# One x tile per block in the v stage, the squares' norms in a tile of their own pool, and another order of the first loads of a 7x7 stage

## The chip, the cores and the metric

The kernel runs on one NeuronCore of a Trainium2 chip. The time is that of one execution on the device, in microseconds (us): the median of three runs. A NeuronCore has five engines with instruction streams of their own: TensorE (PE; its weight loads are PEld in the profile), VectorE (DVE), ScalarE (ACT), GpSimd (POOL) and SyncE (SP). Each carries out its stream in order and waits on semaphores that the others or transfers raise. SP does nothing here but issue transfers (DMAs); ACT and POOL issue some beside their other work. All transfers run on the same 16 DMA engines. PE writes into PSUM, a small memory of banks; everything else lies in SBUF, 128 partitions wide.

## The reference

The input x is (1, 384, 192, 192), all in float32. Two layers follow each other, each `x + layer(group_norm(x))`:

```python
x = x + conv_attention(_gn(x), ...)      # layer 0
x = x + dwconv7x7(_gn(x), symmetrised weight)   # layer 1
# layer 0:
qkv = einsum('bchw,oc->bohw', x, w_qkv)          # 384 -> 1152 channels
qkv = qkv.reshape(b, 3*c, 96, 2, 96, 2).max(axis=(3, 5))   # 2x2 max pool
qkv = depthwise 3x3 convolution of qkv           # 'SAME', 1152 groups
q, k = rows of q and k divided by their norms over all 9216 positions
attn = einsum('bhcn,bhdn->bhcd', q, k)           # 8 heads, 48x48, over channels
out = sum over four k of a_i * topk_softmax(attn, k) @ v
out = upsample2x(gelu(out)); out = einsum with w_proj
```

The norms of q and k need every position, so v is used only after q and k are complete. The second group norm needs all of layer 0's output.

## The kernel before, in words

**Statistics.** x is read once for the first group norm, and the scale is folded into the weights `wq`. Convolutions of the first q/k blocks are begun meanwhile.

**q/k stage** (loop `for b in range(NB + 1)`, NB = 24 blocks of 8 image rows). For each of six channel tiles `pooled` multiplies (L639) into PSUM tile `pq` and pools on DVE into a `ring` tile; one block later `depthwise` runs nine taps on DVE (L680, L682) into `qk`; `products` squares qk on ACT (L691, sums into `ssq`), transposes it on PE (L700), copies it out on ACT (L706) and adds to the Gram matrices (L709). In the last round (b == NB) there is no new block. `convolve` then begins the v convolution (L537) of the first four x tiles from `xv_begun`, two tiles and one channel tile at a time, six calls of twelve matmul passes; they are called after channel tiles 2, 4 and 6, ahead of the last `products`.

**v stage.** A block (NBC = 16) is two rows of every 32, so a block has NT = 6 tiles of 2x192 positions for each of KT = 3 channel tiles. `load_v` loads two of the tiles (UT = 2) by three DMAs on SP (L880); `convolve` multiplies and reduces 2x2 maxima on DVE (L543) into `rows`; `depthwise_v` adds nine taps on DVE (L907 for the first, L903) into `vb`; `attend` multiplies with the attention matrix (L959) and applies gelu on ACT (L966); `project` multiplies with `w_proj` (L983), and ACT writes y (L991). `residual` adds x, loaded once more by `load_r` (L1000), to y in four DVE additions (L1017) into one of three `sx` tiles, squares the sum on ACT (L1037) for the second group norm, and stores it to the DRAM tile `sd` from POOL (L1058, two DMAs of 600 KB) and for edge rows to `sh`. All x tiles, for the convolution and for the residual, come from one pool `xp2` of six buffers with one tag. Three blocks are convolved ahead while `attention` runs, a generator whose steps are called between the convolutions: it makes the norms `rn` from `ssq` (L771 to L781, with one power on POOL), spreads them along the free axis by diagonal tiles `dg` and a matmul (`along_free`, L223 to L225), scales the Gram matrices (L788), ranks the entries on DVE (L813 to L821) and builds the softmax mix. Its tiles are in pool `ap`. Then the loop over i runs in a written order; behind it come the last three blocks without convolutions: all taps still missing, then three rounds of attend, project and residual.

**7x7 stage.** 48 steps of CB = 8 channels. A step n needs `main` (the rows, 1200 KB, from sd), `aux` (edge rows, 600 KB, from sh), `w` (1024 KB) and `h` (256 KB), each with three buffers, filled two steps ahead from ACT's queue; steps 0 and 1 are loaded from SP. POOL's `borders` prepares main and aux, ACT's `columns` and `rest` copy parts of w into h and of main into aux, DVE's `middle` adds the residual's diagonal to w. `h` also gets a row of constants, `offs`, which DVE makes from the second group norm (L1294, L1299) and ACT's queue writes by DMA (L1296, L1300). Then PE takes, for each of eight channels, three matmuls into `pc` (L1389, L1394 with w and main, L1400 with h and aux), and DVE and ACT scale the result out (L1413, L1411); POOL interleaves it (L1359) and SP stores it (L1363). `along` spreads means and scales as above through PSUM tiles of the same tag `pc`.

**What sets the order.** A planner orders each engine's stream by the order in which the program is traced and by when it expects inputs to be ready. `keep` (also given as `pin`) ties an instruction behind the one traced before it on its engine; `with tc.issue_after(ins)` ties a group behind `ins` on its engine. A pool's memory is taken as a stack; a tile of a new pool waits for those who used the memory before. `multiplied` is the last Gram matmul of the latest `products`.

Of the kernel before, what the change touches and what calls it, by code (L numbers as in the profile page):

```python
# [78 lines left out]
def conv_preact_d2(  # L79
# [138 lines left out]
    def along_free(dst, src, pool, name, tag=None):  # L218

        ps = pool.tile([P, C], F32, name=f"af_{name}", tag=tag or f"af_{name}")  # L220
        for t in range(KT):
            dg = const.tile([P, P], F32, name=f"dg_{name}_{t}", tag="dg", bufs=2)
            nc.vector.tensor_scalar_mul(dg, ident, src[:, t : t + 1])  # L223
            nc.tensor.matmul(ps[:, t * P : (t + 1) * P], ones, dg, start=True, stop=True)
# [305 lines left out]
    def convolve(i, t0, ct, xb, pin):  # L530
# [3 lines left out]
        for u in range(UT):  # L534
            for kt in range(KT):
                pin(
                    nc.tensor.matmul(  # L537
                        ps[:, u, 0 : RB * HW], wq[:, kt, o : o + P], xb[:, kt, u, :],
# [12 lines left out]
    with ExitStack() as bx:  # L551
# [172 lines left out]
        for b in range(NB + 1):  # L724
# [3 lines left out]
            else:  # L728
# [3 lines left out]
                xb = xpool.tile([P, KT, 2 * UT, RB * HW], F32, name="xv_begun", tag="xb")  # L732
                for kt in range(KT):
                    nc.sync.dma_start(xb[:, kt], image_rows(kt, order[0], 0, 2 * UT))
            qk = []
            for ct in range(2 * KT + 1):
# [10 lines left out]
                if b > 0 and ct > 0:  # L747
# [3 lines left out]
                    if b == NB and ct % 2 == 0:  # L751
                        for n in range(ct - 2, ct):
                            t0 = n // KT * UT
                            convolve(0, t0, n % KT, xb[:, :, t0 : t0 + UT], lambda ins: ins)
                    if ct == 2 * KT:
                        multiplied = products(b - 1, qk)
            if b == 2:
# [10 lines left out]
    def attention(ap):  # L768

        rn = ap.tile([P, 2 * KT], F32, name="rn")  # L770
# [98 lines left out]
    xp2 = dx.enter_context(tc.tile_pool(name="xp2", bufs=6))  # L869
# [6 lines left out]
    def load_v(i, t0):  # L876
        b = order[i]
        xb = xp2.tile([P, KT, UT, RB * HW], F32, name=f"xv{b}_{t0}", tag="xv")
        for kt in range(KT):
            nc.sync.dma_start(xb[:, kt], image_rows(kt, b, t0, UT))  # L880
# [117 lines left out]
    def load_r(i, ot):  # L998
        xr = xp2.tile([P, NT, RB * HW], F32, name=f"xr{order[i % NBC]}_{ot}", tag="xv")
# [108 lines left out]
    for j, dys in ((NBC - 2, (2,)), (NBC - 1, (0, 1)), (NBC, (0,))):  # L1108
# [3 lines left out]
    for j in range(NBC - 2, NBC + 1):  # L1112
        gl = attend(j, keep)
        after = []
        for ot in range(KT):
# [5 lines left out]
            next(after[ot])  # L1121
        before = after
# [13 lines left out]
    with ExitStack() as ex_:  # L1136
# [24 lines left out]
        def queue(n):  # L1161

            if n < 2:
                return nc.sync.dma_start
            return lambda dst, src: keep(nc.scalar.dma_start(dst, src))
# [34 lines left out]
        ws = {n: load_w(n) for n in range(2)}  # L1200
        ws = {n: (ws[n], load_h(n)) for n in range(2)}
        auxes = {n: load_aux(n) for n in range(2)}
        mains = {n: (load_main(n), auxes[n]) for n in range(2)}
# [91 lines left out]
        for n in ws:  # L1295
            nc.scalar.dma_start(ws[n][1][ONE : ONE + 1], offs[span(n), 0, :])  # L1296
# [184 lines left out]
```

## Time and profile before

| what | value |
|---|---|
| three runs, us | 2817.28, 2816.37, 2819.05 (median 2817.28) |
| the profiled execution, us | 2823.79 |
| its span, first to last instruction, us | 2822.1 |
| mean granted PE clock | 0.987 |
| busy: PE, PEld, DVE, ACT, POOL, us | 2640.9, 1582.7, 2320.9, 870.5, 761.4 |
| moved by DMA | 584.52 MB, 207 GB/s on average |
| q/k stage ends, v stage begins | about 1360 to 1394 us |
| loop of the v stage | blocks of 50.35 us, to 2141 us |
| last three blocks | 2142 to 2217 us |
| 7x7 stage | from 2229.78 us, 48 steps, 11.64 us each |

The profiled execution is 6.5 us longer than the median of the runs; sums made from the profile's durations are made against the profiled execution. Matmuls in float32 appear as two passes each, so "x12" is six matmuls. Times in "start us" are counted from the span's start. In a row of waits the numbers are the total, how often, and the longest. A wait for several semaphores is put down to the one that came last by the profile.

### The profile page before, as it was taken

Reading aid. Unit: us, or ns where it says so; the run is one execution under the profiler, and the core shown is the slowest. Engines: PE = TensorE matmul, PEld = TensorE weight load, DVE = VectorE, ACT = ScalarE, POOL = GpSimd, SP = SyncE. Lnnn points to the kernel's source line nnn. Section 1 sums busy time; section 2 is a strip of 40 time slices with the busy share of each in tenths; the row PEclk is TensorE's granted clock in tenths of the full one; section 3 lists DMA queues with packets and bytes.
Section 4 is the critical chain, followed back from the end, with each engine's and each line's share of the span. In section 5 each row is a group of like instructions: output and inputs, shape, how many; then the busy total and the mean of one; then the engine's idle time right before and its main releaser. Section 6 shows DMA issues by size and latency. Waiting matters only on the chain.

```text
span 2822.1 us, 25467 instructions
## 1 busy us (share of the span) xinstructions
PE 2640.9 (94%) x8671; PEld 1582.7 (56%) x8671; DVE 2320.9 (82%) x3382; ACT 870.5 (31%) x1637; POOL 761.4 (27%) x884
## 2 busy tenths in 40 slices
PE   0399999999999999999999999999998699999997
PEld 0144444444445444444556666666666477777775
DVE  7989887887878878778698888888889678777886
ACT  0141111111111111111202232322324567777775
POOL 1034444100000000000102230100101467888886
PEclk9999999999999999999999999999999799999999
DMA  9976766301001011010235998575666899999997
GB/s 377 400 244 219 258 200 219 126 34 67 34 34 67 34 51 50 34 67 1 80 124 189 332 376 293 199 251 179 235 207 224 301 304 362 372 373 370 373 373 248
DMA packets 236353, 584.52 MB, mean 207 GB/s; under 512 B 16656, under 2 KB 168064, under 8 KB 219456
## 3 DMA queue, kind: packets, MB, share of 16 engines
q1 hardware_dynamic: 175296, 286.77, 29.1%
q0 software_dynamic: 37376, 148.85, 15.2%
q10 hardware_dynamic: 23552, 147.27, 13.9%
q8 instruction: 69, 1.13, 0.2%
q14 instruction: 60, 0.49, 0.0%
HBM read 374.47 MB, written 208.21 MB: 206 GB/s over the span
## 4 chain that ended last, share of the span: by engine, by line
PE 89%; DVE 6%; DMA 3%; POOL 1%; issue 1%; ACT 0%; ACTq 0%; POOLq 0%; SPq 0%; DVEq 0%
PE pq L639 38%; PE pv L537 18%; PE pc L1400 6%; PE pc L1389 6%; PE pc L1394 6%; PE pr L983 4%; PE po L959 3%; DMA xs<-in_x_dram 2%; PE grams L709 2%; PE tr L700 2%; PE pq_begun L423 1%; DVE st L318 1%; DVE vb L903 1%; DVE sx L1017 1%; DMA bp<-in_bproj_dram 1%
## 5 line engine op out<-in xcount | busy, mean ns | idle before, releaser
L639 PE MATMUL pq<-xq,wq 128*128 128x512 f32 x2268 | 990.7, 592 | 0.0
L639 PEld LDWEIGHTS pq<-xq,wq 128*128 128x128 f32 x2268 | 423.2, 190 | 492.0 <-issue 446.8
L682 DVE SCALAR_TENSOR_TENSOR qk<-ring,wd,qk 128x384 f32<-128x384 f32 x1152 | 676.1, 615 | 20.9 <-ACT ring L669 7.1
L537 PE MATMUL pv<-xv,wq 128*128 128x384 f32 x1656 | 540.7, 487 | 3.2 <-DVE rows L543 3.0
L647 DVE TENSOR_REDUCE ring<-pq 128x128 f32<-128x512 f32 x428 | 294.7, 689 | 190.5 <-PE pq L639 188.8
L537 PEld LDWEIGHTS pv<-xv,wq 128*128 128x128 f32 x1656 | 314.8, 190 | 218.3 <-DVE rows L543 5.0
L1413 DVE TENSOR_SCALAR apart<-pc,rb 32x576 f32<-32x576 f32 x384 | 312.0, 813 | 125.7 <-PE pc L1400 111.4
L1411 ACT ACTIVATE apart<-pc,rb 32x576 f32<-32x576 f32 x384 | 281.1, 732 | 144.5 <-PE pc L1400 139.7
L903 DVE SCALAR_TENSOR_TENSOR vb<-rows,wd,vb 128x576 f32<-128x576 f32 x384 | 313.3, 818 | 11.3
L1400 PE MATMUL pc<-aux,h 128*128 128x288 f32 x768 | 250.9, 408 | 2.7 <-POOL aux L1322 2.7
L1389 PE MATMUL pc<-main,w 128*128 128x288 f32 x768 | 251.4, 409 | 0.3 <-issue 0.3
L1394 PE MATMUL pc<-main,w 128*128 128x288 f32 x768 | 251.3, 409 | 0.0
L1017 DVE TENSOR_TENSOR sx<-xr,y 128x576 f32<-128x576 f32 x192 | 217.4, 1173 | 33.8 <-ACT y L991 21.4
L691 ACT ACTIVATE junk<-qk 128x384 f32<-128x384 f32 x144 | 75.3, 523 | 548.8 <-DVE qk L682 548.8
L801 POOL MEMSET lower<- 128x2304 f32 x1 | 2.0, 2017 | 881.1 <-ACT rows L508 881.1
L1359 POOL COPY res<-apart 128x1152 f32<-128x1152 f32 x96 | 210.0, 2222 | 87.2 <-DMA out_dram<-res 61.0
L1058 POOL DMA_DIRECT2D sd<-sx x96 | 72.2, 756 | 491.8 <-DVE sx L1017 474.2
L543 DVE TENSOR_REDUCE rows<-pv 128x192 f32<-128x768 f32 x144 | 137.8, 957 | 54.2 <-PE pv L537 54.1
L1400 PEld LDWEIGHTS pc<-aux,h 128*128 128x128 f32 x768 | 146.3, 191 | 45.5 <-POOL aux L1322 3.5
L1394 PEld LDWEIGHTS pc<-main,w 128*128 128x128 f32 x768 | 146.7, 191 | 41.9
L1389 PEld LDWEIGHTS pc<-main,w 128*128 128x128 f32 x768 | 146.4, 191 | 41.9 <-issue 0.6
L1037 ACT ACTIVATE wq<-sx,negmid 128x1152 f32<-128x1152 f32 x96 | 120.6, 1256 | 96.6 <-DVE sx L1017 92.5
(216 smaller groups left out, 2384.5 us busy)
## 6 DMA issues: line engine op xcount, KB each, us to landing
sd<-sx POOLq DMA_DIRECT2D x96, 600.0 KB, 10.1
xr<-in_x_dram SPq DMA_DIRECT2D x48, 1152.0 KB, 14.1
out_dram<-res SPq DMA_DIRECT2D x192, 288.0 KB, 8.4
main<-sd ACTq DMA_DIRECT2D x46, 1200.0 KB, 9.8
xv<-in_x_dram SPq DMA_DIRECT2D x138, 384.0 KB, 5.4
xq<-in_x_dram SPq DMA_DIRECT2D x21, 2304.0 KB, 8.2
w<-wt ACTq DMA_DIRECT2D x46, 1024.0 KB, 6.6
xs<-in_x_dram SPq DMA_DIRECT2D x24, 1536.0 KB, 15.1
```

The source lines that it names most:

```text
L537: nc.tensor.matmul(ps[:, u, 0 : RB * HW], wq[:, kt, o : o + P], xb[:, kt, u, :], start=(kt == 0), stop=(kt == KT - 1),)
L639: nc.tensor.matmul(ps, wq[:, kt, ct * P : (ct + 1) * P], rows[:, kt, :, g * 64 : (g + 1) * 64], start=(kt == 0), stop=(kt == KT - 1), skip ...
L647: nc.vector.tensor_reduce(t[:, r0 : r0 + PR, 1 + g * 32 : 1 + (g + 1) * 32], ps.rearrange("p (h a w b) -> p h w a b", h=PR, a=2, b=2), AX. ...
L682: nc.vector.scalar_tensor_tensor(dst, src, w, dst, ALU.mult, ALU.add)
L903: pin(nc.vector.scalar_tensor_tensor(dst, src, w, dst, ALU.mult, ALU.add))
L1017: nc.vector.tensor_tensor(bass.AP(flat.tensor, flat.offset + at(e) + a * RUN, [flat.ap[0], [JP, NT], [1, NJ], [at(f) - at(e), 2]],), xq[:, ...
L1359: keep(nc.gpsimd.tensor_copy(res[:, k], apart[:, :, k].rearrange("p e n -> p n e")))
L1389: nc.tensor.matmul(acc, w[:, i, 0:P], main[:, i, :, 0:NJ], start=True, stop=False)
L1394: nc.tensor.matmul(acc, w[:, i, P : 2 * P], main[:, i, :, 1 : 1 + NJ], start=False, stop=False,)
L1400: nc.tensor.matmul(acc, h[:, i], aux[:, i, :, 0:NJ], start=False, stop=True,)
L1411: keep(nc.scalar.mul(dst, src, scale))
L1413: keep(nc.vector.tensor_scalar_mul(dst, src, scale))
```

## The change

*In q/k's last round and in attention.* `along_free` has one `dg` buffer for each of its three diagonal tiles instead of two in all. `rn` comes from the pool `const` instead of `ap`. The begun convolutions are called at other channel tiles: two after the third, two after the fifth, one after the sixth, one after the seventh round, and all under `issue_after(multiplied)`: the first five are tied behind the last Gram matmul of block 22, the sixth behind that of block 23. `xv_begun` has the tile index ahead of the channel tile.

*In the v stage.* One tile `xvs` in a pool `xvp` holds the x of a whole block; `load_v` fills a third of it, with the tile index ahead of the channel tile. `xp2` has three buffers, for the residuals' x alone. For the last block but one of those that are finished (i == NBC - 1) `load_r` returns a view of `xvs`, whose content is still there, and issues no load: three DMAs of 1152 KB fewer. The first three taps of the last block finished, (NBC, ct, 0) for three ct, move from before the last three rounds to behind the second residual of their first round.

*Into the 7x7 stage.* The loads of steps 0 and 1 on SP are tied to the program's order, behind the last `load_r`, and their order is now w 0, h 0, h 1, aux 0, main 0, w 1, aux 1, main 1; before it was w, h, aux, main, each for both steps. The three DMAs of `offs` are issued from SP instead of ACT. In step 0 the first two pairs of channels take their w and main matmuls, eight in all, before the first h and aux matmul; the other steps keep their order.

```diff
-            dg = const.tile([P, P], F32, name=f"dg_{name}_{t}", tag="dg", bufs=2)
+            dg = const.tile([P, P], F32, name=f"dg_{name}_{t}", tag="dg", bufs=KT)
...
-                xb = xpool.tile([P, KT, 2 * UT, RB * HW], F32, name="xv_begun", tag="xb")
+                xb = xpool.tile([P, 2 * UT, KT, RB * HW], F32, name="xv_begun", tag="xb")
                 for kt in range(KT):
-                    nc.sync.dma_start(xb[:, kt], image_rows(kt, order[0], 0, 2 * UT))
+                    nc.sync.dma_start(xb[:, :, kt], image_rows(kt, order[0], 0, 2 * UT))
...
-                    if b == NB and ct % 2 == 0:
-                        for n in range(ct - 2, ct):
-                            t0 = n // KT * UT
-                            convolve(0, t0, n % KT, xb[:, :, t0 : t0 + UT], lambda ins: ins)
                     if ct == 2 * KT:
                         multiplied = products(b - 1, qk)
+                    if b == NB:
+                        with tc.issue_after(multiplied):
+                            for n in ((), (), (0, 1), (), (2, 3), (4,), (5,))[ct]:
+                                t0 = n // KT * UT
+                                convolve(0, t0, n % KT, xb[:, t0 : t0 + UT], lambda ins: ins)
...
-        rn = ap.tile([P, 2 * KT], F32, name="rn")
+        rn = const.tile([P, 2 * KT], F32, name="rn")
...
-    xp2 = dx.enter_context(tc.tile_pool(name="xp2", bufs=6))
+    xp2 = dx.enter_context(tc.tile_pool(name="xp2", bufs=3))
+    xvp = dx.enter_context(tc.tile_pool(name="xvp", bufs=1))
+    xvs = xvp.tile([P, NT, KT, RB * HW], F32, name="xv")
...
-        b = order[i]
-        xb = xp2.tile([P, KT, UT, RB * HW], F32, name=f"xv{b}_{t0}", tag="xv")
+        xb = xvs[:, t0 : t0 + UT]
         for kt in range(KT):
-            nc.sync.dma_start(xb[:, kt], image_rows(kt, b, t0, UT))
+            nc.sync.dma_start(xb[:, :, kt], image_rows(kt, order[i], t0, UT))
...
+        if i == NBC - 1:
+            return xvs[:, :, ot]
+        xr = xp2.tile([P, NT, RB * HW], F32, name=f"xr{order[i % NBC]}_{ot}", tag="xr")
...
-    for j, dys in ((NBC - 2, (2,)), (NBC - 1, (0, 1)), (NBC, (0,))):
+    for j, dys in ((NBC - 2, (2,)), (NBC - 1, (0, 1))):
...
+            if (j, ot) == (NBC - 2, 1):
+                for ct in range(KT):
+                    depthwise_v(NBC, ct, (0,), keep)
...
-            if n < 2:
-                return nc.sync.dma_start
-            return lambda dst, src: keep(nc.scalar.dma_start(dst, src))
+            engine = nc.sync if n < 2 else nc.scalar
+            return lambda dst, src: keep(engine.dma_start(dst, src))
...
-        ws = {n: load_w(n) for n in range(2)}
-        ws = {n: (ws[n], load_h(n)) for n in range(2)}
-        auxes = {n: load_aux(n) for n in range(2)}
-        mains = {n: (load_main(n), auxes[n]) for n in range(2)}
+        ws, mains = {0: load_w(0)}, {}
+        hs = [load_h(n) for n in range(2)]
+        for n in range(2):
+            ws[n] = ws[n] if n == 0 else load_w(n), hs[n]
+            aux = load_aux(n)
+            mains[n] = load_main(n), aux
...
-            nc.scalar.dma_start(ws[n][1][ONE : ONE + 1], offs[span(n), 0, :])
+            nc.sync.dma_start(ws[n][1][ONE : ONE + 1], offs[span(n), 0, :])
...
-        nc.scalar.dma_start(wh[ONE - TOP].rearrange("(t p) n -> p t n", p=P), offs)
+        nc.sync.dma_start(wh[ONE - TOP].rearrange("(t p) n -> p t n", p=P), offs)
...
+            def sums(q, steps):
+                if q not in ahead:
+                    ahead[q] = pc.tile([P, 2, 512], F32, name=f"pc{n}_{q}", tag="pc")
+                for k in range(2):
+                    i = 2 * q + k
+                    for j in steps:
+                        lhs, rhs = (
+                            (w[:, i, j * P : (j + 1) * P], main[:, i, :, j : j + NJ]) if j < 2
+                            else (h[:, i], aux[:, i, :, 0:NJ])
+                        )
+                        keep(
+                            nc.tensor.matmul(
+                                ahead[q][:, k, 0 : NT * NJ], lhs, rhs,
+                                start=(j == 0), stop=(j == 2), skip_group_check=True,
+                            )
+                        )
+                return ahead[q]
+
+            if n == 0:
+                for q in range(2):
+                    sums(q, range(2))
+            for q in range(CP):
+                ps = sums(q, range(2 if q in ahead else 0, 3))
```

More of the change, by code (lines that the diff above doesn't have):

```diff
@@ L537, in convolve @@
                     nc.tensor.matmul(
[L538 removed]
+                        ps[:, u, 0 : RB * HW], wq[:, kt, o : o + P], xb[:, u, kt, :],
                         start=(kt == 0), stop=(kt == KT - 1),
@@ L998, in load_r @@
     def load_r(i, ot):
-        xr = xp2.tile([P, NT, RB * HW], F32, name=f"xr{order[i % NBC]}_{ot}", tag="xv")
+        if i == NBC - 1:
+            return xvs[:, :, ot]
+        xr = xp2.tile([P, NT, RB * HW], F32, name=f"xr{order[i % NBC]}_{ot}", tag="xr")
         nc.sync.dma_start(xr, image_rows(ot, order[i % NBC], 0, NT))
@@ L1382, in conv_preact_d2 @@
             apart = outp.tile([P, CP, 2, NT * NJ], F32, name=f"apart{n}", tag="apart", bufs=3)
-            for q in range(CP):
-                ps = pc.tile([P, 2, 512], F32, name=f"pc{n}_{q}", tag="pc")
+            ahead = {}
+            def sums(q, steps):
+                if q not in ahead:
+                    ahead[q] = pc.tile([P, 2, 512], F32, name=f"pc{n}_{q}", tag="pc")
                 for k in range(2):
                     i = 2 * q + k
-                    acc = ps[:, k, 0 : NT * NJ]
-                    keep(
-                        nc.tensor.matmul(
-                            acc, w[:, i, 0:P], main[:, i, :, 0:NJ], start=True, stop=False
-                        )
-                    )
-                    keep(
-                        nc.tensor.matmul(
-                            acc, w[:, i, P : 2 * P], main[:, i, :, 1 : 1 + NJ],
-                            start=False, stop=False,
-                        )
-                    )
-                    keep(
-                        nc.tensor.matmul(
-                            acc, h[:, i], aux[:, i, :, 0:NJ],
-                            start=False, stop=True,
-                        )
-                    )
+                    for j in steps:
+                        lhs, rhs = (
+                            (w[:, i, j * P : (j + 1) * P], main[:, i, :, j : j + NJ]) if j < 2
+                            else (h[:, i], aux[:, i, :, 0:NJ])
+                        )
+                        keep(
[3 more added lines that the diff above has]
+                            )
+                        )
+                return ahead[q]
[4 more added lines that the diff above has]
+                ps = sums(q, range(2 if q in ahead else 0, 3))
                 c = n * CB + 2 * q
```

## The prediction

> **What bounds the kernel now.** I read the page's chain first, then PE's waits, then the stages in which those waits lie. The chain says who has to be relieved:
>
> ```profile
> PE 89%; DVE 6%; DMA 3%; POOL 1%; issue 1%; ACT 0%; ACTq 0%; POOLq 0%; SPq 0%; DVEq 0%
> ```
>
> PE is the bound, and the other 11% lie where PE is let down. The list of who waited for whom, for PE, names the places (total, times, longest, in us). Leaving out the statistics at the start, which the change does not touch, they are few:
>
> ```profile
> PE po L959 <- DVE vb L903: 5.1, 2, 3.6
> PE af_rk L224 <- DVE dg_rk L223: 3.9, 1, 3.9
> PE pv L537 <- DVE rows L543: 3.0, 1, 3.0
> PE pc L1400 <- POOL aux L1322: 2.7, 1, 2.7
> ```
>
> Next the busy time by stretch (start and end; length; PE, PEld, DVE, ACT, POOL busy; granted PE clock; DMA share; GB/s): one block of the v loop, the moment after the wait of af_rk, the sums at the end of the v stage, the first matmuls of the 7x7 stage.
>
> ```profile
> 1800.25:1850.60 50.35, 50.35 (x173) 32.70 (x173) 44.81 (x51) 13.76 (x30) 4.48 (x6) 1.00 0.63 215
> 1401.09:1404.51 3.42, 3.23 (x9) 2.45 (x10) 1.24 (x4) 0.00 (x0) 0.00 (x0) 0.50 0.84 279
> 2176.00:2217.00 41.00, 22.57 (x96) 16.87 (x94) 33.53 (x35) 27.01 (x57) 10.48 (x14) 0.83 1.01 367
> 2229.00:2241.00 12.00, 8.99 (x20) 5.87 (x20) 4.00 (x8) 3.13 (x3) 7.14 (x11) 0.51 0.73 278
> ```
>
> The v loop is PE without a hole (50.35 of 50.35), so whatever the change does inside it is worth nothing unless it makes PE wait. At the v stage's end PE is half idle and the DMA engines are full (1.01). Around the first and the last of these stretches PE runs at half clock. So the change is priced in three seams.
>
> **Seam 1, from q/k to v (1360 to 1447).** The chain in order of time (start, us):
>
> ```profile
> 1393.02 1.22 ACT rows L508 x5
> 1394.27 2.02 POOL lower L801
> 1396.29 1.33 POOL rn L772
> 1399.08 2.06 DVE dg_rk L223
> 1401.28 1.19 PE af_rk L224 x4
> ```
>
> The squares that rn sums were done on ACT at 1381.1, but rn was reduced at 1394.35, right after the last gram matmul: it waits for memory that the q/k stage still held under pool `ap`, and on POOL it then stands behind the memset of `lower`. In `const` that wait is gone: the reduce can go at 1381, the power (1.36), the maximum (1.0) and the reciprocal (0.2) by about 1385, ten us before PE asks. The third diagonal, which waited 0.76 for PE with two buffers, has its own. PE's 3.89 go, and with them the half clock: 3.23 us of matmul at 0.50, worth 1.6. Attention's comparisons on DVE (15 of 2.55 us) start some ten us earlier, so they needn't be run back to back; the 3.05 wait at 1446.8 comes where three follow each other (1438.40, 1440.95, 1443.41) with no `rows` reduce between. I count it as gone; if the order keeps such a triple, it stays. Together 8.5.
>
> Against it stands the new order of the first six convolutions. Before, twelve of their passes (2, 4, 4 and 2 in PE's timeline from 1361.55 to 1368) filled the holes between the transposes of block 22, whose copies on ACT stand behind squares that wait for DVE (1.84 us idle before 1363.61). Now they are queued behind that block's last gram matmul; nothing else is there for PE, and 12 passes at 0.3225 (the chain has 36 in 11.61) = 3.9 come back as idle time. From both sides: 0 if ACT's order closes up, 3.9 if not; I take 3.9, as the row stands. The sixth convolution moves behind the last gram matmul, a swap that costs PE nothing and brings the grams 3.9 forward; ACT's border fills of `rows2` (18 of 0.26) move behind it and have no reader before block 3 at 1487. **Net 4.6.**
>
> The loads: SyncE's first v load waited for the last depthwise (DVE, 1380.35) and then
>
> ```profile
> SPq L880 <- PE pv L537: 8.1, 1, 8.1
> ```
>
> for the begun convolutions, until 1388.5. The new tile follows a halved xp2 in the stack, so by the pools' sizes it lies over the rings and not over the q/k x tiles: about 8 us earlier. Nothing waited for these loads before; this covers the sixth convolution's move, after which the next input is wanted at once (otherwise 5.4 us from issue to landing would be bare).
>
> **The v loop.** Three loads of 384 KB per pair of tiles as before, the same 1536-byte runs. A third of the tile is free once its own convolution of the previous block is done, 38.6 us before it is wanted (1800.2 to 1838.8), against 5.4 to land; a residual's x comes one block ahead as before, 14.1 against more than 30. DVE has 5.5 us to spare. Zero; without that cover a late load costs PE directly, in 12 blocks.
>
> **Seam 2, the last three blocks (2142 to 2217).** Here DVE sets the end: 33 depthwise taps of 0.82 (27.1), then nine sums of four L1017 at 1.17 started 1.14 apart (4.55 each, 41.0): 2142.0 + 68.1 = 2210.1. The last ended at 2217.0; the 6.9 between are
>
> ```profile
> DVE sx L1017 <- DMA sd<-sx: 5.5, 4, 2.2
> DVE sx L1017 <- ACT wq L1037: 1.5, 1, 1.5
> ```
>
> since sum n+3 needs the buffer of sum n, whose stores take 9 to 12.8 us to land. Moving nine taps (7.4) behind the second sum lets the first two start 7.4 earlier, and the taps run while their stores land. The third sum starts at 2178.2, as before (2177.98), and its store opens the sixth, that one's the ninth. So the gain isn't 7.4: it is what these two stores gain in a full DMA. From 2183 until the sixth store was in, the engines had about 9.6 MB to move (four and a half stores of 1.23, two x loads of 1.18, h and both aux); now 8.3 (the half store and one x load are in earlier, one aux queues behind `main` 0, `w` 0 comes in). 1.3 MB at the row's 367 GB/s is 3.5. Three x loads (3.5 MB) of the kept block go too, but at 2133 to 2157, where they held up nobody. **3.5**, between 0 (the ninth waits as long) and 6.9 (no wait left). What is late next: `w` 0 and `w` 1, loaded at 2159 while the DMA idled, are pinned into the full stretch; 1 MB is 2.9 us, counted above for `w` 0, and `w` 1 goes behind `main` 0.
>
> **Seam 3, into the 7x7 stage.** ACT stood still for the constant's rows, and so the copies for the third tap group came late:
>
> ```profile
> 2231.46 0.62 ACT L1187 COPY h<-w 32x512 f32<-32x512 f32 x1 [13.02 <-DVE offs L1299]
> 2232.53 2.12 ACT L1349 COPY aux<-main 32x2304 f32<-32x2304 f32 x1
> ```
>
> ACT's end (2234.65), and not POOL's as the wait says (borders done 2231.45), released L1400:
>
> ```profile
> 2229.78 1.30 PE L1389 MATMUL pc<-main,w 128*128 128x288 f32 x2 [0.30 <-issue]
> 2234.74 1.30 PE L1400 MATMUL pc<-aux,h 128*128 128x288 f32 x2 [2.70 <-POOL aux L1322]
> 2240.63 0.72 PE L1400 MATMUL pc<-aux,h 128*128 128x288 f32 x2
> 2241.19 0.65 PE L1389 MATMUL pc<-main,w 128*128 128x288 f32 x2
> ```
>
> With the rows on SyncE these copies end near 2228.5, and eight matmuls that need neither aux nor h go first (8 x 0.97 = 7.8 at half clock), so the 2.7 close. The rest is clock. Eight matmuls were done at 2240.63; at full clock (0.485) they take 3.9, so the stage began in effect at 2236.75, 7.0 after its first matmul. The row: the clock rose 5.9 us after PE ran on without a hole (2234.74 to 2240.63). If it does so from the first matmul, the effective start is 2.95 after it: **4.0** gained. The Trainium skill (TensorE: Matmul & The Clock Gate, Part 1: The HAM clock gate) says that about 3.4 us of sustained work, seen in windows that run freely, raise the clock; that is 3.4 to 6.8, mean 5.1, and makes 4.4. I use the row; the bounds are 0 and 7.0. From there PE has no wait but those of `al`, and `main` lands 12 us ahead, so the gain lasts to the end.
>
> A rule speaks against it. The Trainium skill (DMA: Bandwidth & Descriptors, Queues, rings and completion order) says that each of SyncE's rings is consumed in order. The rows are now queued behind `w` 1, `aux` 1 and `main` 1 (2.9 MB), which wait behind `main` 0. On ACT's own queue the row took 1.9 us (2228.47 to 2230.36); by the rule it lands after `main` 1, which with 4.1 MB ahead including the last store is near 2228, plus 2: 2230. With this seam 3.5 earlier, the first L1400 wants it 6.9 after 2226.3, at 2233. Both fit; by the rule only 3 us are left.
>
> **The sum.** 4.6 + 3.5 + 4.0 = 12.1. The profiled execution took 2823.79 (span 2822.1 and 1.7 around it), which becomes 2811.7; it is 6.5 above the median 2817.28, and I take the difference over: **2805.2** (by the clock rule 2804.8).
>
> **The rivals.**
> *Seam 1 gives nothing* (0.22): af_rk is queued where it waits all the same, or the transposes leave more idle than 3.9 and the clock falls. For it: only the planner's order decides, and ACT's row. Time: 2817.3 - 7.5 = 2809.8.
> *The stores rule* (0.17): the DMA at 1.01 is the bound up to 2229, the ninth sum waits as before, and the constant's row behind `main` 1 hands PE a new wait. For it: 20.9 MB instead of 18.8 must pass. Against: they start 7.3 us earlier. Only seam 1 counts: 2812.7.
> *More than that* (0.08): no idle at block 22 (8.5), no wait in the sums (6.9), the early clock (5.3): 2796.6.
> *Slower* (0.07): loads wait for the whole x tile and not for their third. Then block i+1's first load is issued only when PE has finished block i, and PE waits some 6 us (three issues and 5.4), 12 times: 72, so 2877. It decides from 1.0 us a block. Against it: `main`<-`sd` was issued at 2216.07, while later stores into `sd` landed to 2228.8, so waits go by region there.
> My forecast keeps 0.46, with 2801 to 2809 as its own range.
>
> **The numbers.** No change can be told within 0.2% (5.6 us). Faster: nearly all of 0.46, 0.7 of the first rival, a third of the second, all of the third: 0.74; within: 0.19; slower: 0.07. The range leaves out the slower case and the far end of the high gain: 2797 to 2814.
>
> **What would show it.** Right: no wait of af_rk and no half clock near 1401; PE holes of about 4 us before 1369; nine sums ending near 2213.5; ACT's h and aux copies done before POOL's borders; L1400 never waiting, the clock up within 7 us of the first `pc`; the v loop still 50.35 a block. Wrong: a period above 50.35, waits on `xv` loads, `main` 1 or the constant's row after 2233, or a new wait of PE between 1369 and 1500.

## The result and the profile after

The changed kernel takes 2807.85 us in the median of eight runs (2802.46 to 2811.43), the kernel before 2818.33 beside it (2815.36 to 2824.11): a ratio of 0.9961, 95% interval 0.9951 to 0.9972, 10.5 us. Two later comparisons on other occasions gave 0.9957 (0.9945 to 0.9969) and 0.9955 (0.9938 to 0.9972), 14.0 and 13.3 us in the medians. The forecast was 12.1.

Two profiled executions mislead here. Their spans are 2822.1 and 2800.7, 21.4 apart, twice the difference of the medians. So the trace is cut at the same instructions in both, and the changed kernel is profiled twice more. The figures are the length in us from one matmul to the next named one (the last pq, the last pv and the end of a step are ends, the others starts; `gs` is the matmul that sums for the second group norm):

| stretch | before | after, three profiles (after, e4, e11) |
|---|---|---|
| start to first transpose of q/k | 233.4 | 227.9, 232.9, 232.6 |
| to last pq | 1126.9 | 1125.6, 1127.1, 1127.0 |
| to first po (seam 1) | 137.60 | 132.90, 132.89, 132.89 |
| to last pv (v loop) | 643.10 | 643.10, 643.10, 643.10 |
| to gs, the last sums (seam 2) | 78.14 | 75.80, 75.39, 75.58 |
| to first pc | 10.55 | 10.33, 10.32, 10.31 |
| to the end of step 0 (seam 3) | 18.85 | 13.99, 14.37, 14.19 |
| step 3 of the 7x7 stage | 18.88 | 14.19, 14.21, 14.21 |

(Steps 1 and 2 lie between the last two rows, 11.64 each in all four.) The rows of the three seams repeat within 0.5 us in the three profiles of the changed kernel, and they give 4.7 + 2.6 + 0.2 + 4.7 = 12.2 us. Of the kernel before there is one profile. In the runs below that keep its code in a seam, seam 1 took 139.51 once (e3: the clock was at half for 10.2 us there instead of 3.4) and seam 2 took 77.50 and 78.95 (e1, e3), so a seam of before is known to 1 or 2 us. The start and step 3 are not counted. Step 3 depends on whether the clock falls to half there, and the code does not decide that: the old 7x7 stage took 14.20 in e1 and 18.41 in e2, the new one 17.5 to 17.6 in e3, e5, e6 and e8 and 14.2 to 14.3 in the other seven profiles of it. How often each kernel pays for it is not known.

PE's waits in the kernel after, leaving out the start (some rows are left out, marked by dots):

```profile
PE gs L185 <- DVE about L205: 12.5, 1, 12.5
PE po L961 <- DVE vb L905: 5.2, 2, 3.6
PE al L1277 <- DVE al_dg L1276: 4.7, 4, 1.9
...
PE pc L1408 <- POOL aux L1333: 2.3, 1, 2.3
...
PE pv L537 <- DVE rows L543: 1.4, 1, 1.4
```

The wait of `af_rk` is gone, that of pv for `rows` is 1.4 instead of 3.0, and the wait inside the first pc step has turned into one ahead of it (2.3). The same stretches as before, by engine (start and end; length; PE, PEld, DVE, ACT, POOL busy; granted PE clock; DMA share; GB/s):

```profile
1788.69:1839.04 50.35, 50.35 (x173) 32.68 (x173) 44.82 (x51) 13.80 (x30) 4.50 (x6) 1.00 0.61 212
1395.00:1401.00 6.00, 4.63 (x15) 2.54 (x14) 6.00 (x4) 1.29 (x6) 0.30 (x1) 1.00 1.06 401
2164.40:2205.20 40.80, 22.71 (x98) 17.00 (x96) 34.35 (x51) 28.44 (x60) 13.24 (x20) 0.85 0.90 320
2214.90:2226.90 12.00, 11.24 (x38) 8.57 (x39) 5.43 (x8) 6.07 (x8) 8.17 (x14) 0.79 0.96 379
```

The v loop's block is 50.35 as before, PE keeps its full clock at the v stage's begin, and in the first 12 us of the 7x7 stage PE is busy for 11.24 instead of 8.99 at a clock of 0.79 instead of 0.51.

**Seam 1** in PE's order of time:

```profile
1353.37 2.15 PE L700 MATMUL tr<-ident,qk 128*128 128x128 f32 x13
1356.54 0.44 PE L700 MATMUL tr<-ident,qk 128*128 128x128 f32 x2 [1.02 <-DVE qk L682]
1357.61 1.90 PE L709 MATMUL grams<-qkT,qkT 128*128 128x144 f32 x12 [0.64 <-ACT qkT L706]
1359.35 0.82 PE L700 MATMUL tr<-ident,qk 128*128 128x128 f32 x6
1360.41 1.08 PE L709 MATMUL grams<-qkT,qkT 128*128 128x144 f32 x6 [0.24 <-ACT qkT L706]
1361.33 19.51 PE L537 MATMUL pv<-xv_begun,wq 128*128 128x384 f32 x60
...
1385.37 0.94 PE L224 MATMUL af_rk<-dg_rk,ones 128*128 128x128 f32 x6
...
1400.10 15.10 PE L537 MATMUL pv<-xv,wq 128*128 128x384 f32 x46 [1.37 <-DVE rows L543]
```

The transposes of block 22 have the holes that the convolutions used to fill, 1.9 us of them; `af_rk` is bare of any wait; and a wait of 1.37 stands at 1400. DVE shows its cause: two comparisons stand in a row ahead of the `rows` reduce that PE waits for, the first of them 4.80 us long instead of 2.55,

```profile
1391.90 4.80 DVE L814 TENSOR_TENSOR gt<-att 128x2304 f32<-128x2304 f32 x1
1396.63 2.55 DVE L816 TENSOR_TENSOR eq<-att 128x2304 f32<-128x2304 f32 x1
1399.10 0.95 DVE L543 TENSOR_REDUCE rows<-pv 128x192 f32<-128x768 f32 x1
```

while POOL worked on `lower` and `diag`:

```profile
1391.82 2.47 POOL L803 TENSOR_SCALAR_AFFINE_SELECT lower<-lower 128x2304 f32<-128x2304 f32 x1
1394.23 1.07 POOL L848 MEMSET diag<- 128x1152 f32 x1
```

**Seam 2**, DVE's sums from the third on (four to a sum):

```profile
2166.36 4.62 DVE L1022 TENSOR_TENSOR sx<-xr,y 128x576 f32<-128x576 f32 x4
2170.81 9.02 DVE L1022 TENSOR_TENSOR sx<-xv,y 128x576 f32<-128x576 f32 x8
2183.98 4.63 DVE L1022 TENSOR_TENSOR sx<-xv,y 128x576 f32<-128x576 f32 x4 [4.14 <-DMA sd<-sx]
2189.73 10.02 DVE L1022 TENSOR_TENSOR sx<-xr,y 128x576 f32<-128x576 f32 x9 [1.12 <-DMA sd<-sx]
```

The third starts 36.83 after the last pv matmul (before: 36.89). The waits for stores are as large in total as before (5.3 against 5.5), but there are two instead of four: 4.14 ahead of the sixth sum and 1.12 ahead of the seventh.

**Seam 3**, PE from the last `al`:

```profile
2212.55 0.80 PE L1277 MATMUL al<-al_dg,ones 128*128 128x128 f32 x2 [1.07 <-DVE al_dg L1276]
2215.66 6.23 PE L1408 MATMUL pc<-main,w 128*128 128x288 f32 x16 [2.31 <-POOL aux L1333]
2221.72 2.10 PE L1408 MATMUL pc<-aux,h 128*128 128x288 f32 x8
2223.66 1.13 PE L1408 MATMUL pc<-main,w 128*128 128x288 f32 x4
```

and ACT beside it:

```profile
2216.44 0.62 ACT L1195 COPY h<-w 32x512 f32<-32x512 f32 x1 [11.85 <-DVE w L1264]
2217.08 0.40 ACT L1196 COPY h<-w 32x256 f32<-32x256 f32 x1
2217.51 2.12 ACT L1360 COPY aux<-main 32x2304 f32<-32x2304 f32 x1
```

ACT no longer waits for `offs` but stands still almost as long (11.85 instead of 13.02), now for DVE's addition of the diagonal to w (0.03 us lie between that addition's end and the first copy; in before it was 0.87).

### The profile page after: what moved, and what is told of

It reads as the page before. It is cut to its first block, busy times and chain, and to the rows that moved or that the text cites. A ratio compares the mean times of both kernels' runs of the same rounds, so it can differ in the third digit from the quotient of the medians.

```text
span 2800.7 us, 25536 instructions
## 1 busy us (share of the span) xinstructions
PE 2632.7 (94%) x8671; PEld 1577.0 (56%) x8671; DVE 2313.1 (83%) x3382; ACT 872.5 (31%) x1637; POOL 757.2 (27%) x884
## 4 chain that ended last, share of the span: by engine, by line
PE 85%; DMA 7%; DVE 5%; ACT 1%; POOL 1%; issue 1%; ACTq 0%; SPq 0%; POOLq 0%; DVEq 0%
PE pq L639 38%; PE pv L537 19%; PE pc L1408 15%; PE pr L985 4%; PE po L961 3%; DMA out_dram<-res 3%; DMA xs<-in_x_dram 2%; PE grams L709 2%; PE tr L700 2%; PE pq_begun L423 1%; DVE st L318 1%; DVE vb L905 1%; DVE sx L1022 1%; DMA sd<-sx 1%; DMA main<-sd 1%
## 5 line engine op out<-in xcount | busy, mean ns | idle before, releaser
L1408 PE MATMUL pc<-main,w 128*128 128x288 f32 x1536 | 436.7, 407 | 2.5 <-POOL aux L1333 2.3
L1022 DVE TENSOR_TENSOR sx<-xr,y 128x576 f32<-128x576 f32 x180 | 203.7, 1175 | 27.2 <-ACT y L993 21.4
L1063 POOL DMA_DIRECT2D sd<-sx x96 | 72.4, 758 | 487.4 <-DVE sx L1022 469.5
L985 PE MATMUL pr<-gl,wp 128*128 128x288 f32 x576 | 142.7, 406 | 0.0
L1264 DVE SCALAR_TENSOR_TENSOR w<-eye,sb,w 128x512 f32<-128x512 f32 x96 | 133.6, 1430 | 1.5
## 6 DMA issues: line engine op xcount, KB each, us to landing
xs<-in_x_dram SPq DMA_DIRECT2D x24, 1536.0 KB, 15.3
```

The lines of the kernel that those rows point to most:

```text
L985: nc.tensor.matmul(ps[:, 0:H], wp[:, ct, ot * P : (ot + 1) * P], gl[:, ct, h * H : (h + 1) * H], start=(ct == 0), stop=(ct == KT - 1),)
L1022: nc.vector.tensor_tensor(bass.AP(flat.tensor, flat.offset + at(e) + a * RUN, [flat.ap[0], [JP, NT], [1, NJ], [at(f) - at(e), 2]],), xq[:, ...
L1408: nc.tensor.matmul(ahead[q][:, k, 0 : NT * NJ], lhs, rhs, start=(j == 0), stop=(j == 2), skip_group_check=True,)
```

## The experiments

Each run was timed beside the kernel before on its own chip: e1 to e4 together, e5 to e8, e9 to e12. "Seams" are the four stretches of the table above, from last pq to first po, from last pv to gs, on to first pc, and to the end of step 0.

| run | ratio to before (95%) | seams |
|---|---|---|
| e1 seam 1, old tiles | 0.9996 (0.9988, 1.0003) | 137.57, 77.50, 10.56, 18.77 |
| e2 seams 1 and 2 | 0.9975 (0.9963, 0.9986) | 132.88, 74.58, 8.08, 19.80 |
| e3 seam 3 alone | 1.0000 (0.9990, 1.0010) | 139.51, 78.95, 11.58, 14.94 |
| e4 after again | 0.9957 (0.9945, 0.9969) | 132.89, 75.39, 10.32, 14.37 |
| e5 taps back | 0.9968 (0.9957, 0.9979) | 132.89, 78.54, 10.61, 14.17 |
| e6 diagonal first | 0.9959 (0.9947, 0.9971) | 134.35, 75.29, 8.08, 13.86 |
| e7 nothing ahead | 0.9961 (0.9949, 0.9972) | 132.88, 75.57, 10.33, 16.53 |
| e8 old call places | 0.9941 (0.9929, 0.9953) | 130.38, 75.96, 10.33, 13.78 |
| e9 e8 with e6 mended | 0.9950 (0.9932, 0.9968) | 130.45, 75.42, 10.23, 13.46 |
| e10 e9, diagonals early | 0.9936 (0.9918, 0.9954) | 130.28, 75.55, 10.24, 13.53 |
| e11 after, third time | 0.9955 (0.9938, 0.9972) | 132.89, 75.58, 10.31, 14.19 |
| e12 rows on ACT | 0.9957 (0.9942, 0.9973) | 132.88, 75.64, 10.32, 14.06 |

The times of a kernel spread by 4 to 17 us, so a run's ratio decides 2 to 5 us; smaller amounts are read from the seams.

**e1, the first seam on the old tiles.** The kernel before with `rn` in const, three `dg`, the new call places, and

```diff
-xb = xp2.tile([P, KT, UT, RB * HW], F32, name=f"xv{b}_{t0}", tag="xv")
+xb = xp2.tile([P, UT, KT, RB * HW], F32, name=f"xv{b}_{t0}", tag="xv")
```

> Edit: the kernel before with the first seam's part alone (rn in the constants, one diagonal per tap of af_rk, the six begun convolutions behind block 22's products), but on the old six x tiles, which lie over the q/k x tiles. Theory (the new tile's place is what lets the sixth convolution move): the first load of v waits for the sixth convolution, which the trace of after ends at 1390.8 on PE; with 5.4 to 6.3 us from issue to landing PE stands bare for about 5.5 us and the gain of this seam in the trace of after (4.7 us from the end of pq to the first po) is eaten: 2818.3 minus 0, within 2 us of before, and PE's list shows a wait of some 5 us of pv on the xv loads near 1391. Rival (the place of the tile is worth nothing, loads are early anyway): 4.7 faster, 2813.6, no such wait.

Measured: no gain, seam 1 at 137.57. PE's waits have

```profile
PE pv L537 <- DMA xv<-in_x_dram: 3.6, 1, 3.6
```

and the six passes behind it took 4.18 us, at half clock. The theory holds, with 3.6 bare instead of 5.5 and the clock on top: SyncE issued the load at 1393.04, right after the sixth convolution had ended (1392.96). In before no engine waited for these loads, so the tile's new place alone should earn nothing (that was not tried), but without it the moved sixth convolution eats the whole seam.

**e2, the v stage alone; e3, the 7x7 stage alone.** Each takes the hunks of the diff up to, or from, `queue(n)`.

> Edit: the first and second seam (everything the change does up to the ninth sum), with the 7x7 stage's loads, rows and matmul order as before. Theory (the seams add up): 4.7 from the first and 2.4 from the second, as the two traces give them between the same matmuls, so 2818.3 - 7.1 = 2811.2; L1400's wait for aux of 2.7 us stays. Rival (the second seam's gain comes from the load order of the 7x7 stage, which is as before here): 4.7 alone, 2813.6, and the ninth sum ends no earlier relative to the last pv matmul than before. Rival (what the profiles show of both is chance of the clock): within 1.5 us of before.

> Edit: the 7x7 stage's part alone (load order, constant's rows from SyncE, eight matmuls ahead); the v stage is that of before. Theory: 4.9 us, the difference of the two traces from the first pc to the end of step 0: 2813.4. Rival (the 4.7 us that step 3 also lost, a half clock window and shorter waits for al, belong to this part too and aren't chance): 9.6, 2808.7, and no half clock window in steps 2 and 3 of this profile. Rival (the constant's row comes late behind the main load): within 1.5 us of before and a wait of the first pc<-aux,h matmul.

e2 gained 8.3 us in the medians. Seam 1 gave its 4.7, seam 2 3.6 at the old load order, and the first pc came 2.5 earlier behind gs, which nobody had expected: DVE's first addition to w began 0.41 us ahead of POOL's copy into aux there and took 0.90, as it does in e6 below. Inside step 0 the wait for ACT grew to 4.5 and took 1.0 back. e3 gained nothing that can be told: from gs to the end of step 0 it is 2.9 faster, but step 1 took 12.5 instead of 11.64, and the 2.0 us that are left lie inside the interval of its ratio (2.8 either way). Its profile also lost 1.9 us in seam 1, whose code is that of before, to the clock. Its rival with 9.6 is out: step 3 was at 17.5 here. So the 7x7 part alone is at most worth 2.8, and the whole needs both stages.

**e4 and e11, the same kernel again.**

> Edit: none, the kernel after once more, to see what differs between two profiles of one kernel. Theory (of the 21.4 us between the two profiled spans 12.1 belong to the change and some 9 to chance: 6.9 before the end of pq and 4.7 in step 3, less 2.3 in the later steps): median again near 2807.9, and this profile is some 5 us longer than the first, with the same 132.9 us from the end of pq to the first po, 643.1 of v loop, and 14.0 for step 0, but other numbers before the first transpose (227.9 in the first profile, 233.4 before) and in step 3 (14.2 against 18.9). Rival (those two belong to the change): first transpose near 228 and step 3 near 14.2 again, and the median 2802.

> Edit: none, the kernel after beside the two above, for their comparison. Both theories: a ratio to before of 0.996, as in the first two times (0.9961 and 0.9957); the fixed parts again at 132.9 (end of pq to first po), 643.1 (v loop), 75.4 to 75.8 (last pv to gs), 10.3 (gs to first pc).

The seams repeated; the start did not (232.9 and 232.6); step 3 did, at 14.2, and the median of e4 was 2803.44 instead of 2807.9, though the ratio to before held. That the start differs by chance is shown here. For step 3 it is not: all three profiles of the changed kernel have 14.2, against this run's theory, and only runs of other kernels (e1 against e2, e12 against e8) speak for chance.

**e5, the nine taps back ahead of the three rounds.**

```diff
-for j, dys in ((NBC - 2, (2,)), (NBC - 1, (0, 1))):
+for j, dys in ((NBC - 2, (2,)), (NBC - 1, (0, 1)), (NBC, (0,))):
...
-            if (j, ot) == (NBC - 2, 1):
-                for ct in range(KT):
-                    depthwise_v(NBC, ct, (0,), keep)
```

> Edit: the kernel after with the nine taps of the last block back ahead of the three rounds. Theory (the taps' place is the second seam's gain): last pv to gs takes 78.1 us again, as in the three profiles with the old place, instead of 75.4; 2.8 us slower than after. Rival (the gain comes from the kept x tile, three loads fewer, and the load order): 75.4, same time as after.

Seam 2 was 78.54, as with the old place. So the taps' place is the gain; the kept x tile and the new load order together give none.

**e6, the additions of the diagonal first.** The list of waits puts the 2.31 ahead of the first pc on POOL's copy. But in all profiles up to here the first weight load started 0.07 us after the end of DVE's first addition (`middle`, L1264), which writes a part of w that the first tap reads.

```diff
         along(sb, std1, 0)()
-        middle(0)
+        spread_rb = along(rb, rstd1, 0)
+        centred = middle(0)
...
-        along(rb, rstd1, 0)()
-        for kt in range(1, KT):
-            nc.vector.tensor_scalar_mul(offs[:, kt, :], ones, off1[:, kt : kt + 1])
+        with tc.issue_after(centred):
+            spread_rb()
+            for kt in range(1, KT):
+                nc.vector.tensor_scalar_mul(offs[:, kt, :], ones, off1[:, kt : kt + 1])
```

> Edit: the kernel after with DVE's first two additions of the residual's diagonal (middle of step 0) ahead of the second and third row of constants and of the copy of rb. Theory (the first pc matmul is released by the first of these two additions, 0.07 us after its end in all six profiles, although the list of waits names POOL's copy into aux; the additions stood behind 1.1 us of other work and then beside POOL's copy, which stretched the first from 0.74 or 0.90 to 1.97): the first pc starts 8.1 us after gs instead of 10.3, and step 0 ends up to 2.2 earlier; if the constant's row or ACT's copies take it back, a wait of the first pc<-aux,h of about as much. Rival (POOL's copy into aux is what the first pc waits for, as the list says): 10.3 again, no gain.

The first pc came 8.08 after gs, with no wait, and while POOL's copy still ran (2215.70 to 2218.15):

```profile
2215.29 3.41 DVE L1264 SCALAR_TENSOR_TENSOR w<-eye,sb,w 128x512 f32<-128x512 f32 x2
2215.70 2.45 POOL L1336 COPY aux<-main 32x2304 f32<-32x2304 f32 x1
2215.43 0.79 PE L1278 MATMUL al<-al_dg,ones 128*128 128x128 f32 x2 [1.07 <-DVE al_dg L1277]
2216.29 6.10 PE L1411 MATMUL pc<-main,w 128*128 128x288 f32 x16
...
2233.21 0.72 PE L1411 MATMUL pc<-aux,h 128*128 128x288 f32 x2 [2.09 <-POOL main L1324]
```

So the list had named the wrong engine. The time was not better, for step 1 took 15.66: the constants' last store (192 KB into `wh`) was issued 11.1 us behind gs instead of 7.7, at 2219.32, and landed at 2224.68. (It is 3.4 later behind gs and 5.6 later behind the first pc; the expectation of e9 below has 6.) ACT's next `h` load reads what it wrote and stood in ACT's stream until then, ahead of all that follows:

```profile
2224.70 0.53 ACTq L1173 DMA_DIRECT2D h<-wh  x1
...
2226.97 2.97 ACT L1429 ACTIVATE apart<-pc,rb 32x576 f32<-32x576 f32 x4 [5.05 <-DVE apart L1431]
2229.95 2.12 ACT L1363 COPY aux<-main 32x2304 f32<-32x2304 f32 x1
2232.09 0.61 ACT L1195 COPY h<-w 32x512 f32<-32x512 f32 x1
2232.71 0.40 ACT L1196 COPY h<-w 32x256 f32<-32x256 f32 x1
```

and PE went on 0.1 after the last of these had ended (2233.11), and soon at half clock. Seam 1, whose code is that of after, took 1.5 us more here (134.35), because the clock fell to half for 3.4 us at block 22.

**e7, the eight matmuls ahead taken out.**

```diff
-            if n == 0:
-                for q in range(2):
-                    sums(q, range(2))
```

> Edit: the kernel after without the eight matmuls ahead in step 0 (every channel takes its three in turn as before). Theory (the eight matmuls are what covers the late copies and the constant's row; the row lands 0.57 us after the second main load, because it is queued behind it): the first pc<-aux,h waits until ACT's copy into aux is done, 4.0 us after the first pc, so about 2.0 us of bare wait, and the clock's rise starts again: step 0 (first pc to its end) takes 18 instead of 14.2 us. Rival (the rows' move to SyncE alone closes that wait, as the prediction's row of 13.02 us for ACT had it): no wait above 0.5 us, step 0 below 15.

```profile
2222.08 2.26 PE L1408 MATMUL pc<-main,w 128*128 128x288 f32 x4 [2.31 <-POOL aux L1333]
2226.13 1.30 PE L1408 MATMUL pc<-aux,h 128*128 128x288 f32 x2 [1.79 <-ACT aux L1360]
```

The wait is back, 1.79, and step 0 takes 16.53: the eight matmuls are worth 2.3 us, less than the 3.8 of the theory. Its half about the copies holds.

**e12, the constant's rows back on ACT's queue**, two calls of `nc.sync` to `nc.scalar`.

> Edit: the kernel after with the constant's rows back on ACT's queue, all else as in after. Theory (SyncE's ring is consumed in order: from there the last row landed 0.54 to 0.60 us after the second main load in seven profiles, 2.9 to 6.3 us after its issue): from ACT's queue it lands about 2.2 us after its issue, while the second main load is still on its way; the total stays within 1 us of after, since eight matmuls cover either. Rival (the full DMA and not the ring made the row late): it lands 4 to 6 us after its issue here too. Rival of the prediction (the rows on ACT hold its copies up by what the 13.02 us row promised): ACT's copy into aux ends 4 us later and a wait of that size stands at the first pc<-aux,h.

All seams are those of after, and ACT's copy into aux ended 3.96 us behind the first pc (after: 3.97). The rows' move is worth nothing in this order of DVE's work. (In before and in e2, with the rows on ACT, DVE made the last of them behind its additions to w, and ACT's copies began 0.87 and 1.07 us behind the additions; in after and here DVE makes them ahead, and it is 0.03.) The constants go out in three transfers, and the theory took the last for all. This one, 192 KB into `wh`, took from ACT's queue

```profile
wh<-offs ACTq DMA_DIRECT2D x1, 192.0 KB, 6.0
```

as long as it took from SyncE in the run of e11,

```profile
wh<-offs SPq DMA_DIRECT2D x1, 192.0 KB, 6.3
```

and landed 0.32 behind `main` 1, as it landed 0.54 to 0.60 behind it from SyncE in after, e3, e4, e5, e7, e8, e9 and e11 (e6 and e10: 3.1). So for it the theory fell and the first rival holds. But it is not what step 0 reads. That is the first transfer, 4 KB into `h` 0; the views give it no landing, the last update of its semaphore in the traces does. From SyncE it came 7.6 us after its issue and 0.2 behind `main` 1 (after, e4, e11; in e9 and e10 0.5 to 0.6 ahead of it), from ACT's queue 5.4 after its issue and 2.1 ahead of `main` 1. For this row the queue seems to matter, as the theory had it (e12 is one profile), and PE gained nothing by it, since its first third tap came 5.1 us later still (2227.00).

**e8, the old call places.** The kernel after, with

```diff
-                    if b == NB:
-                        with tc.issue_after(multiplied):
-                            for n in ((), (), (0, 1), (), (2, 3), (4,), (5,))[ct]:
+                    if b == NB and ct % 2 == 0:
+                        for n in range(ct - 2, ct):
```

ahead of `products`, as before the change.

> Edit: the kernel after with the six begun convolutions called where they were (two after the second, fourth and sixth channel tile, tied to nothing); rn stays in the constants, the diagonals stay three, the tiles stay where they are. Theory of the prediction (rn's memory alone takes the wait of af_rk away, and the new order costs 3.9 us of holes at block 22, of which the profile of after shows 1.9): the end of pq to the first po takes 131 us or a little less instead of 132.9. Rival (with the convolutions spent in those holes PE has nothing to do while the norms' chain of the last block runs, and the wait of af_rk is only moved): 133 to 137.6, a wait of PE near af_rk again, perhaps with a half clock window.

```profile
1355.02 1.50 PE L700 MATMUL tr<-ident,qk 128*128 128x128 f32 x10
1356.36 0.81 PE L537 MATMUL pv<-xv_begun,wq 128*128 128x384 f32 x2
1357.01 0.49 PE L700 MATMUL tr<-ident,qk 128*128 128x128 f32 x3
1357.33 1.46 PE L537 MATMUL pv<-xv_begun,wq 128*128 128x384 f32 x4
...
1388.21 0.71 PE L224 MATMUL af_rk<-dg_rk,ones 128*128 128x128 f32 x4 [0.25 <-DVE rn L781]
...
1402.81 12.52 PE L537 MATMUL pv<-xv,wq 128*128 128x384 f32 x38 [1.24 <-DVE rows L543]
```

Seam 1 is 130.38: the new places of the calls cost 2.5 us, and the rest of the seam's change (`rn` in const, three diagonals, the x tile's new place) gives 7.2. `af_rk` waits 0.25.

**e9 and e10.** e9 is e8 with `middle(0)` ahead of rb's copy and all three rows of constants ahead of both; e10 makes the diagonals of steps 2 and 3 in the middle of the step:

```diff
+                    if 1 < n < KT + 1:
+                        dgs = [diagonal(v, n - 1) for v in (mean1, std1, rstd1)]
```

> Edit: the kernel after with the old calls of the begun convolutions (as in e8) and, in step 0 of the 7x7 stage, the second and third row of constants made ahead of DVE's additions of the diagonal, and rb's copy behind them, so that neither the additions nor the row's store is late. Theory (e8's 2.5 us at block 22 is there again; e6 lost its 2.2 because the rows' store, made 6 us later, held up ACT's next load, then ACT's copies and step 1): end of pq to first po 130.4, gs to first pc 8.5 instead of 10.3, step 1 at 11.64, about 4 us faster than the kernel after on the same chip. Rival (what e6 lost was the second main load, which is as late here): step 1 longer than 13 us again, and only e8's 2.5 are left.

> Edit: e9 and, in steps 2 and 3, the three diagonals for the spread means and scales made on DVE in the middle of the step instead of at its end. It goes beyond the change. Theory (in those steps PE waits 1.2 to 1.9 us for a diagonal each time, and in six of ten profiles the clock then ran a window of 3.4 us at half rate, 3.3 us more in step 3): both waits go, 2.6 us, and with them most of the half clock windows, so 3 to 5 us faster than e9, and step 3 at 13 us or less. Rival (PE then waits for the copies that free the PSUM tiles): steps 2 and 3 as before, same time as e9.

e9 kept e8's 2.5 and had no trouble in step 1, but against the 4 us expected it is 1.7 faster than e11 in the medians, less than the two can tell apart. Its first pc came at 10.23 and not at 8.5: the two additions,

```profile
2212.75 3.50 DVE L1263 SCALAR_TENSOR_TENSOR w<-eye,sb,w 128x512 f32<-128x512 f32 x2
```

started within 0.01 us of POOL's copy (2212.76, 2.10 long), and the first took 2.66. In e6 it had started 0.41 ahead of the copy and took 0.90. e10's rival holds: steps 3 and 4 take 14.21 and 14.06, for PE now waits for what frees the PSUM tiles,

```profile
PE al L1282 <- DVE apart L1435: 2.3, 2, 1.2
```

and its median, 2.75 below e9's, lies within both intervals. Step 1 took 13.48 in it: the 192 KB store landed only at 2223.09, 10.2 us after its issue and for a reason that is not known, and ACT's next `h` load stood until then, as in e6. Against the kernel after (e11) on the same chip, e10 is 4.4 us faster in the medians (2801.89, all runs 2799.78 to 2804.22, against 2806.33, all runs 2804.37 to 2810.68). Its ratio is the lowest here, though e8's interval overlaps it, and it beats both kernels. Of its gain over after, 2.6 us (seam 1) and 0.7 (step 0) are seen in the trace, against 1.8 lost in step 1 and 0.65 in its v loop (643.75); the rest is open.

## Why the prediction was right

**The total.** 12.1 forecast; 12.2 by the seams, and 10.5, 14.0 and 13.3 in medians. It was made against the profiled execution and carried over to the median; had it been checked against the second profile alone, it would have looked 9 us short. Its parts were less good than its sum: seam 2 was 0.9 too high and seam 3 0.9 too low, and that these cancel is luck. Two of its readings need a word. It is the second and the last of its four stretches that stand at half clock (0.50 and 0.51), not the first. And its list of PE's waits is a choice: `gs` (15.3) and `al` (6.6) are longer than all in it.

**Seam 1: 4.6 forecast, 4.7 measured, by two errors that cancel.** The wait of `af_rk` and its half clock went, as computed; DVE reduced `rn` at 1374.01, which is the 1381 of the forecast less the 6.9 us by which this profile is ahead at the last pq. "I count it as gone" of the 3.05 wait for `rows` failed: 1.4 stayed, for two comparisons still follow each other (1.24 in e8, where neither was stretched). "12 passes at 0.3225 = 3.9 come back as idle time" was too dear: 1.9 of holes in the trace, 2.5 by e8. 8.5 - 1.4 - 2.5 = 4.6. The aside that the early tile covers the sixth convolution's move was right: e1 shows the load bare, and the gain gone. The first rival's fear that the clock falls in those holes came true once, in e6 (1.5 us).

**The v loop: zero, measured 643.10 to 643.10** (up to 643.85 in e7 to e10). PE waits for no `xv` load, and the slower rival is out.

**Seam 2: 3.5 forecast, 2.6 measured** (2.3 to 2.7; 3.6 in e2). The mechanism was right to the store: the third sum started where it was said to, its store, in at 2183.86, opened the sixth at 2183.98. But that one's store did not bind the ninth: it was in at 2197.2, and the ninth started at 2198.58, straight behind the eighth. It ended 73.6 after the last pv matmul; the forecast made that 72.4, before it was 75.9. The mis-sized term is "1.3 MB at the row's 367 GB/s": the third sum's store took 12.6 us to land (10.7 before), with `w` 0 issued 0.6 behind it. e2 has the loads in their old order, both `w` in by 2157.2, ahead of the third sum (2168.6). There the store took 10.3, the ninth sum ended at 72.40, as forecast, and the seam gave 3.6. So the new order of the loads costs seam 2 about 1 us; which of them does was not tried.

**Seam 3: 4.0 forecast, 4.9 measured from gs on, with a wrong reason in it.** The failed step is "ACT stood still for the constant's rows, and so the copies for the third tap group came late". They end 4.0 behind the first pc now, 4.9 before, and later (2219.63) than POOL's borders (2217.83), against the list of signs. Of ACT's 13.02 only the last 0.87 was the rows': until then the next thing that was late, DVE's addition to w, held it as well. e12 shows the move of the rows to be worth nothing once DVE makes them early. What closed the 2.7 is the eight matmuls (e7: 2.3). The clock rose earlier than the row said, and that is the mis-sized term. The granted clock of 0.79 over the 12 us from 2214.90 means 5.0 us at half rate, to 2219.9, which is 4.3 after the first pc; in e4 and e11 it was 5.0 and 4.7, in e6, e8, e9, e10 and e12 3.2 to 4.4. The row's 5.9 is high. The estimate of 3.4 to 6.8 that the forecast made from the Trainium skill (TensorE: Matmul & The Clock Gate, Part 1: The HAM clock gate) holds all but e9 (3.2) and e10 (3.3), and its mean of 5.1 was the better guess.

The rule on rings gave the right place for the row that step 0 reads: it came in 0.2 behind `main` 1, at 2218.94, and 2.8 us were left to the first third tap (2221.72) where the text had 3. e12 supports it, for from ACT's queue the same row came in ahead of `main` 1. It does not explain the 192 KB store, which came in behind that load from either queue. The same section of the Trainium skill (DMA: Bandwidth & Descriptors, Queues, rings and completion order) also says that a transfer's semaphore increment lands only after every earlier write of that DMA engine, across its queues; the store's 0.32 in e12 fits that sentence, and no run here tests it.

**The rivals.** *Seam 1 gives nothing* and *the stores rule* are out by the seams; *more than that* would have needed the holes closed, which e8 does in part.

## What to carry to other kernels

Cut two traces at the same instructions before you explain a difference, and profile a kernel twice: here two profiled executions lay 21 us apart, where the medians and the seams give 10 to 14. When a row shows an engine waiting for X, look up what else its next instruction needs: behind X stood something nearly as late, and taking X away was worth nothing. Work tied behind a critical chain "to get it out of the way" is paid for where it used to fill holes.

## What the runs showed of the hardware

- DVE's first addition took 0.74 us away from POOL's copy, 0.90 when it began 0.41 ahead of it, 1.95 to 2.67 when it began with it or during it (each time it ended about 0.55 after the copy), and a comparison 4.80 instead of 2.55 beside POOL's select. The Trainium skill (SBUF — State Buffer, SBUF: two separate sides) calls the pair of ports that the two share a lock which whoever starts first holds for the whole instruction; e6 agrees, and in e9 the two starts lie 0.01 apart, too close to say who was first. The forecast had left this out; between e6 and after, order and lock together moved the first pc by 2.2 us.
- In all fourteen profiles the first pc's weight load starts 0.07 us after the end of DVE's first addition, whatever the list of waits names (POOL's copy in ten, "issue" or nothing in four).
- A 192 KB store took 6.0 us from ACT's queue and 6.3 from SyncE's, with a 1200 KB load under way on SyncE's; 2.2 in the kernel before, where none was. A 4 KB row took 5.4 from ACT's queue and 7.6 from SyncE's, where it stood behind that load.
- The clock falls to half without a long pause of PE. In e6 PE's waits at block 22 were 1.02 and 0.64 us, and it was busy for 1.64 of these 3.41 us (columns as in the stretches above):

```profile
1356.73:1360.14 3.41, 1.64 (x10) 1.10 (x10) 3.38 (x8) 1.75 (x6) 0.00 (x0) 1.00 0.00 0
1360.14:1363.55 3.41, 3.41 (x16) 3.32 (x14) 3.41 (x8) 2.03 (x8) 0.00 (x0) 0.50 0.00 0
```

The clock of all fourteen traces changes only on a grid of 3.41 us. Between 300 and 2780 us, the stretches of this grid after which it fell had PE busy for at most 0.51 of their length, and the least busy one after which it stayed at full rate had 0.41. In after the same two waits fall into two stretches with 2.44 and 2.60 us busy, and the clock stays. So where the grid lies, which differs between executions, can decide about a half clock window, as in step 3.
